# A Mamba block with a mixture of experts: the last chunk's rows in expert tiles, four running sums, and short chunks scanned in pairs of blocks

## The chip, the core and the metric

The kernel runs on one core of a Trainium2 chip. The core has five engines with a queue of instructions each: PE (matrix products), DVE (VectorE), ACT (ScalarE), POOL (GpSimd) and SP (SyncE, which here only issues DMAs). They run side by side and meet at semaphores. Sixteen DMA engines move data between HBM and the on-chip memory SBUF. The metric is the device time of one execution in microseconds; lower is better.

## What is computed

For 4096 rows of 256 values: a Mamba layer with residual and layer norm, then an expert layer with residual and layer norm. Cut to what matters (plain numpy shapes: L = 4096, D = 256, inner width 512, 16 states, 32 experts of width 128, 6 per row):

```python
# Mamba: project, causal convolution of 4 taps, silu, then the scan
dt = softplus(x_conv @ W_dt.T + b_dt)
Bm, Cm = x_conv @ W_B.T, x_conv @ W_C.T          # 16 values a row each
def step(h, inp):                                # h: [512, 16]
    h = exp(dt_t[:, None] * A) * h + dt_t[:, None] * B_t * u_t[:, None]
    return h, h @ C_t                            # y_t
x = layernorm(x + (y * silu(z)) @ W_out.T)

# experts: softmax router, the best 6 of 32, weights scaled to a sum of 1
shared = silu(x @ sg.T) * (x @ su.T) @ sd.T
for e in the six experts of a row:
    out_row += weight[row, e] * (silu(gate_e @ row) * (up_e @ row)) @ down_e
x = layernorm(x + out + shared)
```

All arithmetic is float32.

## The kernel before

**Chunks.** The rows are cut into nine chunks (`SIZES`, L92): a short one of 256 rows, seven of 512, a short one of 256. The channel axis lies on the partitions in four blocks `m` of 128, so a scan unit is one state and one block: `units` (L935) lists chunk, group `g` of two blocks, state `n`, block `i`. A chunk has 64 units.

**One unit** (the loop at L1031): ACT writes the decay `exp(dt * A)` into a PSUM tile `h` (`exp_at`, L961, two units ahead), POOL writes `du` = `u` times the row `b` (`du_at`, L953, four units ahead), DVE scans along the rows (L1066, start value `hlast`) and multiplies by the row `c` (L1070, into `hc`), PE adds `hc` to `y` through a transposing product (`summed`, L980), ACT keeps the last column for the next chunk (`keep`, L972). SP fetches rows `b` and `c` broadcast to all partitions (`load_bc`, L941), two pairs of units ahead.

**Threads.** All else runs as Python generators in `threads`; each unit calls `step()`, which advances every thread to its next `yield`. So the order of instructions on each engine is fixed when the program is built, and a thread's work is spread over the units. Beside the units of chunk `c` run: `front(c + 1)` (projections, convolution, `dt`), `tail(c - 1)` (gate, `W_out`, norm, then `prepare`: router, top 6, shared expert), and expert tiles of chunk `c - 2`.

**Tiles.** `ranked` (L395) gives each (row, expert) a place in a list of tiles of 128 rows, each of one expert; `copies` (L521) issues on POOL six indirect DMAs per 128 rows, which put the rows into the DRAM list `xs`. `SLOTS` (L108) is the number of tiles that the list needs at most, `full[c]` (L113) how many are surely full after chunk `c`; `stage(c)` (L693) lists the tiles that become full then. `tiles` (L671) starts a pair of tiles every `gap` steps; `loaded` (L566) issues its DMAs on SP (rows `xt`, weights `wt`, and expert weights `gu`, `dn`), `pair` (L643) or `pair_of` (L1110) computes it: transpose, gate and up product, tanh, down product, and `added` (L625): ACT scales the result by the row's weight (`yt`, two buffers), and POOL adds it to the output rows in DRAM by an indirect DMA that accumulates. Adds to one copy of the sums must follow each other, so there are three copies, `acc[0..2]` (`LANES`, L102), taken in turn: L635, `acc[(j + i) % LANES]`. `prepare` writes the shared expert's result plus the residual into `acc[0]` (L389). `blanked` (L239) and `cleared` (L252) write zeros into `xs` and `acc` beforehand.

**The last chunk** does not go through tiles. After the scan, `fw.wall` (L1108) takes the weights of all 32 experts (`walls`, L1202). Tiles of chunk 7 that are left are `EARLY` = 8 pairs with weights of their own, and 36 pairs that read from `wall` at an index held in a register. `dense` (L1214) runs every expert over all 256 rows of the last chunk (`expert`, L1176), with the weight of each row, broadcast by `weights` (L1149), zero where the expert was not chosen; it stops at expert 14 (`HALF`) until the tiles are done.

**The finish** (`finish`, L1236) takes two chunks at a time: three loads per chunk from the three copies, two DVE additions, the norm, a store. The next two chunks' loads are issued after the stores.

**PSUM.** Tiles for PE results come from `bank()`, three banks (`BANKS`); `room()` makes a thread wait at build time until one is free.

Of the kernel before, what the change touches and what calls it, by code (L numbers as in the profile page):

```python
# [60 lines left out]
def kernel(  # L61
# [32 lines left out]
    AT = [sum(SIZES[:c]) for c in range(NC)]  # L94
# [7 lines left out]
    LANES = 3  # L102

    AHEAD = 2
    BANKS = 3


    SLOTS = (L - SIZES[-1]) * TOP_K // P + E - 1  # L108
# [3 lines left out]

    full = [max(0, (AT[c + 1] * TOP_K // P - (E - 1)) // 2 * 2) for c in range(NC - 1)]  # L113
    full[NC - 2] = SLOTS

# [13 lines left out]
    held = [0]  # L129

    def room():
        while held[0] >= BANKS:
            yield

    def bank(name):
        held[0] += 1
        return ps_m.tile([P, T], F32, tag="mm", name=name)
# [3 lines left out]

    threads = []

# [85 lines left out]

    xs = dr1.tile([(SLOTS + 1) * P, RW], F32, tag="xs", name="xs")  # L230
    acc = [dr1.tile([L + P, D], F32, tag=f"acc{i}", name=f"acc_{i}") for i in range(LANES)]

    def bound(c):

        return AT[c + 1] * TOP_K // P + E - 1 if c < NC - 2 else SLOTS + 1

# [30 lines left out]
    def prepare(c):  # L267
# [69 lines left out]
        if c < NC - 1:  # L337
            yield from ranked(c, mask)
# [31 lines left out]
        if c == NC - 1:  # L370
            return
# [23 lines left out]
    def ranked(c, mask):  # L395
# [31 lines left out]
        if c < NC - 2:  # L427
            nc.vector.tensor_scalar(down, pc, -half, BIG, ALU.add, ALU.add)
            nc.vector.tensor_scalar_add(down, down, -BIG)
        else:  # L430
            nc.vector.tensor_copy(down, up)
# [89 lines left out]
    def copies(c, at):  # L521

        row, n = row_of[c], 0
        for b in range(blocks(c)):
            for k in range(TOP_K):
                yield
                n += 1
                if n % 3 == 0:
                    yield
                i = nc.gpsimd.indirect_dma_start(  # L530
# [77 lines left out]
    def turned_rows(j, xt):  # L608
        yield from room()
# [15 lines left out]
    def added(j, po, wt, no):  # L625

        yt = q2.tile([P, 2, D], F32, tag="yt", name=f"yt_{j}")
# [4 lines left out]
        for i in range(2):  # L632
            yield
            a = nc.gpsimd.indirect_dma_start(  # L634
                out=acc[(j + i) % LANES],  # L635
                out_offset=bass.IndirectOffsetOnAxis(ap=no[:, i : i + 1], axis=0),
                in_=yt[:, i, :],
                in_offset=None,
                compute_op=ALU.add,
            )  # L640
            adds.append(a.ins)

    def pair(j, xt, wt, gu, dn):  # L643
# [4 lines left out]
        for h in range(2):  # L648
            for i in range(2):
                for k in range(KD):  # L650
# [3 lines left out]
                    )  # L654
        yield
# [10 lines left out]
        for i in range(2):  # L666
            nc.tensor.matmul(po[:, i, :], hm[:, i, :], dn[i], start=True, stop=True)  # L667
        yield
        yield from added(j, po, wt, no)

    def tiles(c, gap, js, weights, one):  # L671
# [3 lines left out]
        if c == NC - 2:  # L675
            yield from rounds(4)
        st, going = {}, []
        for i in range(len(js) + AHEAD if js else 0):

# [17 lines left out]
    EARLY = 8  # L697


    with ExitStack() as c1:  # L700
# [4 lines left out]
        qw = c1.enter_context(tc.tile_pool(name="qw", bufs=6))  # L705
# [41 lines left out]
        nc.vector.memset(hlast, 0.0)  # L747

# [139 lines left out]
        def tail(c):  # L888
# [45 lines left out]

        units = [  # L935
            (c, g, n, i) for c in range(NC) for g in range(G) for n in range(NS)
            for i in range(2)
        ]
        PER = G * NS * 2

        def load_bc(s, which):  # L941
            if s >= len(units) // 2:
                return
            c, g, n, _ = units[2 * s]
            t = p3.tile(
                [P, T], F32, tag="bc"[which] + "b", name=f"{'bc'[which]}b_{c}_{g}_{n}"
            )[:, : SIZES[c]]
            nc.sync.dma_start(
                t, bcd_of[c][2 * n + which : 2 * n + which + 1, :].partition_broadcast(P)
            )  # L950
            (c_of if which else b_of)[s] = t

        def du_at(q):  # L953
            if q >= len(units):
                return
            c, g, n, i = units[q]
            du = p3.tile([P, T], F32, tag="du", name=f"du_{q}", bufs=6)[:, : SIZES[c]]
            nc.gpsimd.tensor_mul(du, u_of[c][:, 2 * g + i, :], b_of[q // 2])  # L958
            du_of[q] = du

        def exp_at(q):  # L961
            if q >= len(units):
                return
            c, g, n, i = units[q]
            m = 2 * g + i
            h = ps_a.tile([P, T], F32, tag="h", name=f"h_{q}")[:, : SIZES[c]]
            nc.scalar.activation(  # L967
                h, dt_of[c][:, m, :], AF.Exp, scale=aneg[:, m, n : n + 1]
            )
            h_of[q] = h  # L970

        def keep(q):  # L972
            c, g, n, i = units[q]
            if c + 1 < NC:
                m = 2 * g + i
                nc.scalar.copy(hlast[:, n, m : m + 1], h_of[q][:, SIZES[c] - 1 : SIZES[c]])  # L976
# [3 lines left out]
        def summed(q):  # L980

            c, g, n, i = units[q]
            nb = blocks(c)
            if n == 0 and i == 0:
# [5 lines left out]
            for b in range(nb):  # L990
                nc.tensor.matmul(  # L991
                    y_of[c, g][b // 2][:, b % 2, ts(i, P)], hc[:, ts(b, P)], ident,
                    start=(n == 0 and i == 0 and b % 2 == 0),
                    stop=(n == NS - 1 and i == 1 and b % 2 == 1),
                    is_transpose=True,
                )
# [32 lines left out]
        exp_at(1)  # L1029
        load_expert_constants()  # L1030
        for q, (c, g, n, i) in enumerate(units):  # L1031
            if q % PER == 0:
# [11 lines left out]
                if 0 < c < NC - 1:  # L1044
# [4 lines left out]
                if c == NC - 1:  # L1049
                    early = tiles(NC - 2, 3, stage(NC - 2)[:EARLY], qw, pair)  # L1050
# [3 lines left out]
            if q % 4 == 0 and 0 < c < NC - 1:  # L1054
# [10 lines left out]
            m = 2 * g + i  # L1065
# [3 lines left out]
            hc = p3.tile([P, T], F32, tag="hc", name=f"hc_{q}", bufs=6)[:, : SIZES[c]]  # L1069
            nc.vector.tensor_mul(hc, h, c_of[q // 2])  # L1070
            hc_of[q] = hc

            if q and n == 0 and i == 0:
# [4 lines left out]
            if q > 1 and n == 0 and i == 1:  # L1078
# [4 lines left out]
            if q % PER == PER - 6:  # L1083
                drain(*mains)
            if q % PER == PER - 1 and 0 < c < NC - 1:
# [7 lines left out]
        drain(last_tail, late, early)  # L1093
# [3 lines left out]
    f2 = ctx.enter_context(tc.tile_pool(name="f2", bufs=2))  # L1097
    f3 = ctx.enter_context(tc.tile_pool(name="f3", bufs=3))
    ps_o = ctx.enter_context(tc.tile_pool(name="ps_o", bufs=1, space=PSUM))
    ps_g = ctx.enter_context(tc.tile_pool(name="ps_g", bufs=3, space=PSUM))  # L1100
    EG = 4
    last = NC - 1
    nb, Tc = blocks(last), SIZES[last]
    row, x1T, hms = row_of[last], x1T_of[last], hms_of[last]
    sums = [ps_o.tile([P, T], F32, tag=f"o{b}", name=f"o_{b}")[:, :D] for b in range(nb)]

    GU = KD * 2 * P
    wall = fw.tile([P, E, GU + D], F32, tag="wall", name="wall")  # L1108

    def pair_of(j, xt, wt, es, _):  # L1110
# [4 lines left out]
        for i in range(2):  # L1115
            for k in range(KD):
# [4 lines left out]
                )  # L1121
        yield
# [22 lines left out]
        yield from added(j, po, wt, no)  # L1145

    columns, through = {}, []

    def weights():  # L1149

        yield from room()
        pw = bank("pw")
        for b in range(nb):
            nc.tensor.transpose(pw[:E, ts(b, P)], row[:, b, WT:RW], ident)
        yield
        ct = f2.tile([E, T], F32, tag="ct", name="ct", bufs=1)[:, :Tc]
        nc.scalar.copy(ct, pw[:E, :Tc])
        free()
        yield
        cd = dram.tile([E, T], F32, tag="cd", name="cd", bufs=1)[:, :Tc]  # L1160
        nc.sync.dma_start(cd, ct)
        yield
        for e in range(0, E, EG):
            while e >= 3 * EG and e - 2 * EG - 1 not in done_with:
                yield
            cb = f2.tile([P, EG, T // 2], F32, tag="cb", name=f"cb_{e}", bufs=3)
# [171 lines left out]
```

## Time and profile before

| | us |
|---|---|
| runs of the kernel (three) | 1987.65 median, 1987.5 to 1989.53 |
| profiled execution, device time | 1985.42 |
| its span, first to last instruction | 1983.7 |

Busy time over that span:

| engine | busy us | share |
|---|---|---|
| PE matmul | 1431.5 | 72% |
| PE weight load | 1025.8 | 52% |
| DVE | 1509.9 | 76% |
| ACT | 995.2 | 50% |
| POOL | 1185.7 | 60% |

The DMA queues moved 362.98 MB; q1 (issued by SP) took 54.1% of the sixteen engines' time and q0 (issued by POOL) 14.7%. The scan of the first short chunk begins at 47.4 us, that of the first long one at 157.3, that of the last short one at 1475.9; the last scan starts at 1632.3. The `W_out` product of the last chunk ends at 1640.9. The first add of the 36 last pairs starts at 1737.4, the last add lands at 1875.4.

A profile row of a group reads: line, engine, operation, output and inputs with shapes, count; then busy time and the mean of one in ns; then the time that the engine stood idle just before, and for what. A row of a window reads: the window and its length, then busy time and count per engine, the clock granted to PE (1 is full), the share of the DMA engines in use and the bytes per second. A group of a helper's line can mix shapes; a chain of waits lists, in order of time, start and length of each piece that held up the next.

### The profile page before, as it was taken

The page shows a single profiled execution, that of the slowest core. Times are in us where ns is not written, and L with a number is a line of the kernel's source. Part 1 is how long each engine was busy: PE and PEld are TensorE (multiplying, and loading weights), DVE is VectorE, ACT ScalarE, POOL GpSimd, SP SyncE. Part 2 cuts the span into 40 slices and gives each one's busy share as a digit, 9 for nine tenths or more (in the row PEclk, how much of TensorE's full clock was granted, in tenths as well). Part 3 has the DMA queues.
Part 4 walks back from the last instruction along what each step waited for, and adds up shares of the span by engine and source line. Part 5 has one row for each costly group of instructions (what it writes and reads, how often), then busy time and mean ns, then how long its engine had stood idle before and what let it go on. Part 6 is the DMA issues. An engine that isn't in the chain of part 4 may idle for free. (4 is left out here: it accounts for less than half of the span.)

```text
span 1983.7 us, 25634 instructions
## 1 busy us (share of the span) xinstructions
PE 1431.5 (72%) x6674; PEld 1025.8 (52%) x6674; DVE 1509.9 (76%) x2572; ACT 995.2 (50%) x2220; POOL 1185.7 (60%) x986
## 2 busy tenths in 40 slices
PE   5958556874876598669866987586656658899745
PEld 4325334533544365456545655575545547777544
DVE  3598899899889989996999799889977752322265
ACT  4566454644555465555654565455545324155333
POOL 1345556467556756795688568957884784087600
PEclk8868775985897599879887999798878879999877
DMA  8329535444744597778786878687857879988753
GB/s 238 82 74 327 163 109 179 131 110 150 220 114 126 171 267 183 210 168 255 194 204 171 249 207 214 173 241 209 234 132 202 194 165 245 296 144 137 133 185 112
DMA packets 334978, 362.98 MB, mean 183 GB/s; under 512 B 64816, under 2 KB 270480, under 8 KB 334832
## 3 DMA queue, kind: packets, MB, share of 16 engines
q1 hardware_dynamic: 293552, 306.85, 54.1%
q0 software_dynamic: 39168, 54.45, 14.7%
q8 instruction: 54, 0.88, 0.2%
q14 instruction: 92, 0.75, 0.1%
q10 hardware_dynamic: 2112, 0.05, 0.1%
HBM read 257.80 MB, written 103.42 MB: 182 GB/s over the span
## 5 line engine op out<-in xcount | busy, mean ns | idle before, releaser
L958 POOL TENSOR_TENSOR du<-u,bb 128x512 f32<-128x512 f32 (+1 forms) x576 | 716.0, 1294 | 447.6 <-DVE h L1066 245.1
L1066 DVE TENSOR_TENSOR_SCAN h<-h,hlast,du 128x512 f32<-128x512 f32 (+1 forms) x576 | 671.0, 1165 | 52.1 <-POOL du L958 25.9
L991 PE MATMUL y<-ident,hc 128*128 128x128 f32 x2048 | 380.8, 321 | 205.6 <-DVE hc L1070 199.2
L991 PEld LDWEIGHTS y<-ident,hc 128*128 128x128 f32 x2048 | 284.9, 165 | 328.4 <-DVE hc L1070 256.3
L1070 DVE TENSOR_TENSOR hc<-h,cb 128x512 f32<-128x512 f32 (+1 forms) x576 | 364.4, 633 | 98.1 <-DMA cb<-bcd 52.0
L634 POOL DMA_INDIRECT acc<-yt,no x212 | 334.3, 1577 | 168.6 <-ACT yt L629 104.3
L967 ACT ACTIVATE h<-dt,aneg 128x512 f32<-128x512 f32 (+1 forms) x576 | 370.8, 644 | 70.9 <-DVE hc L1070 51.0
L976 ACT COPY hlast<-h 128x1 f32<-128x1 f32 x512 | 80.8, 158 | 424.2 <-DVE hc L1070 423.5
L530 POOL DMA_INDIRECT xs<-row,at x180 | 187.3, 1041 | 70.9 <-issue 35.0
L667 PE MATMUL po<-dn,hm 128*128 128x256 f32 x280 | 91.9, 459 | 137.2 <-issue 73.6
L651 PE MATMUL pg<-xsT,gu 128*128 128x128 f32 x1120 | 152.1, 294 | 4.2 <-ACT xsT L617 4.2
L651 PEld LDWEIGHTS pg<-xsT,gu 128*128 128x128 f32 x1120 | 148.9, 212 | 8.9 <-ACT xsT L617 4.7
L667 PEld LDWEIGHTS po<-dn,hm 128*128 128x128 f32 x280 | 57.6, 222 | 165.0 <-issue 85.5
L629 ACT ACTIVATE yt<-po,wt 128x256 f32<-128x256 f32 x212 | 88.2, 467 | 82.4 <-DMA acc<-yt,no 56.1
L829 PE MATMUL pd<-u,w_dt 128*128 128x512 f32 (+1 forms) x288 | 120.4, 564 | 1.0 <-ACT e L835 1.0
L793 PE MATMUL pv<-xin,taps 128*128 128x512 f32 (+1 forms) x288 | 117.5, 551 | 1.7 <-ACT hlast L976 1.5
L1126 DVE SCALAR_TENSOR_TENSOR gt<-gt,pg 128x256 f32<-128x256 f32 x36 | 15.2, 422 | 104.0 <-ACT gt L1124 101.3
L614 PE MATMUL pt<-ident,xt 128*128 128x128 f32 x424 | 66.6, 280 | 22.7 <-DVE row L929 5.5
L829 PEld LDWEIGHTS pd<-u,w_dt 128*128 128x128 f32 x288 | 54.8, 197 | 49.6 <-issue 44.3
L1174 PE MATMUL o<-wall,hm_all 128*128 128x256 f32 x128 | 38.9, 434 | 57.3 <-DVE hm_all L1195 57.3
L793 PEld LDWEIGHTS pv<-xin,taps 128*128 128x128 f32 x288 | 52.8, 192 | 45.5 <-issue 40.3
L782 PE MATMUL px<-xT,w_in 128*128 128x512 f32 (+1 forms) x144 | 69.3, 609 | 6.0 <-DVE row L929 5.3
(205 smaller groups left out, 2067.2 us busy)
## 6 DMA issues: line engine op xcount, KB each, us to landing
bb<-bcd SPq DMA_DIRECT2D x224, 256.0 KB
cb<-bcd SPq DMA_DIRECT2D x224, 256.0 KB
gu<-in_gate_up_t_dram SPq DMA_DIRECT2D x140, 256.0 KB
xs<-blank SPq DMA_DIRECT2D x52, 578.0 KB
xt<-xs SPq DMA_DIRECT2D x212, 128.5 KB
dn<-in_down_t_dram SPq DMA_DIRECT2D x140, 128.0 KB
out<-acc SPq DMA_DIRECT2D x21, 512.0 KB
bb<-bcd SPq DMA_DIRECT2D x64, 128.0 KB
```

The lines of the kernel that those rows point to most:

```text
L530: i = nc.gpsimd.indirect_dma_start(out=xs, out_offset=bass.IndirectOffsetOnAxis(ap=at[:, b, k : k + 1], axis=0), in_=row[:, b, :], in_offs ...
L629: nc.scalar.mul(yt[:, i, :], po[:, i, :], wt[:, i : i + 1])
L634: a = nc.gpsimd.indirect_dma_start(out=acc[(j + i) % LANES], out_offset=bass.IndirectOffsetOnAxis(ap=no[:, i : i + 1], axis=0), in_=yt[:, ...
L651: nc.tensor.matmul(pg[:, h, i, :], gu[i][:, k, ts(h, P)], xT[:, i, k, :], start=(k == 0), stop=(k == KD - 1),)
L667: nc.tensor.matmul(po[:, i, :], hm[:, i, :], dn[i], start=True, stop=True)
L793: nc.tensor.matmul(pv, taps[:, m, k, :], xin[:, m, k : k + Tc], start=(k == 0), stop=(k == TAPS - 1),)
L829: nc.tensor.matmul(pd, w_dt[:, k, ts(m, P)], u[:, k, :], start=(k == 0), stop=(k == M - 1),)
L958: nc.gpsimd.tensor_mul(du, u_of[c][:, 2 * g + i, :], b_of[q // 2])
L967: nc.scalar.activation(h, dt_of[c][:, m, :], AF.Exp, scale=aneg[:, m, n : n + 1])
L991: nc.tensor.matmul(y_of[c, g][b // 2][:, b % 2, ts(i, P)], hc[:, ts(b, P)], ident, start=(n == 0 and i == 0 and b % 2 == 0), stop=(n == NS ...
L1066: nc.vector.tensor_tensor_scan(h, h, du_of.pop(q), hlast[:, n, m : m + 1], ALU.mult, ALU.add)
L1070: nc.vector.tensor_mul(hc, h, c_of[q // 2])
```

## The change

Three things change at once.

1. **The last chunk's rows go to tiles like all others.** `ranked` and the shared expert's store run for every chunk; `SLOTS` and `full` cover all nine chunks. `weights`, `expert`, `dense` and `second` are gone. The tiles of chunk 7's stage all run as early pairs with weights of their own, and `pair_of` runs the pairs of the last stage.
2. **Four copies of the sums.** `added` takes a parameter `lane`: `pair` adds to copies 0 and 1, `pair_of` to copies 2 and 3. Beside the last tiles, `halfway` loads copies 0 and 1 and adds them into the SBUF tile `sums`. `finish` now takes four blocks of 128 rows, adds copies 2 and 3 (loaded into the space of `wall`), normalizes and stores; eight of these run staggered by one step.
3. **Short chunks scan two blocks in one instruction.** A unit of a short chunk covers both blocks of a group: 512 columns, the first block's 256 rows and then the second's. `joined` writes the second block's start into its first column (`du` becomes decay times `hlast` plus `du`, the decay becomes zero), so that the scan restarts there. A short chunk has 32 units, and each calls `step()` twice.

Smaller edits: `take` and `give` count buffers in use when the program is built; the end of the scan waits for the `W_out` product and for chunk 6's tiles only, so that weight loads mix with early pairs; five more PSUM banks serve the last stage; a put of `copies` waits for another POOL instruction since the put before, or issues a tiny `memset` (`apart_from`); chunk 7's puts lose their extra `yield`.

```diff
-    LANES = 3
+    LANES = 4
-    SLOTS = (L - SIZES[-1]) * TOP_K // P + E - 1
+    SLOTS = L * TOP_K // P + E - 1
...
-    full = [max(0, (AT[c + 1] * TOP_K // P - (E - 1)) // 2 * 2) for c in range(NC - 1)]
-    full[NC - 2] = SLOTS
+    full = [max(0, (AT[c + 1] * TOP_K // P - (E - 1)) // 2 * 2) for c in range(NC)]
+    full[NC - 1] = SLOTS
...
-        if c < NC - 1:
-            yield from ranked(c, mask)
+        yield from ranked(c, mask)
...
-                if n % 3 == 0:
+                if n % 3 == 0 and c < NC - 2:
                     yield
+                while apart_from[0] and c < NC - 1:
+                    yield
+                if apart_from[0]:
+                    nc.gpsimd.memset(between, 0.0)
+                apart_from[0] = True
...
-    def added(j, po, wt, no):
+    def added(j, po, wt, no, lane):
+        yield from take("yt", 2)
...
-                out=acc[(j + i) % LANES],
+                out=acc[lane + (j + i) % 2],
...
+        def joined(q):
+            if q >= len(units) or not short(units[q][0]):
+                return
+            n, m, k = state(q)
+            Tc = SIZES[units[q][0]]
+            first, du = h_of[q][:, Tc : Tc + 1], du_of[q][:, Tc : Tc + 1]
+            nc.scalar.activation(
+                du, first, AF.Identity, bias=du, scale=hlast[:, n, m + 1 : m + 2]
+            )
+            nc.scalar.copy(first, zero)
...
-                    early = tiles(NC - 2, 3, stage(NC - 2)[:EARLY], qw, pair)
+                    early = tiles(NC - 2, 3, stage(NC - 2), qw, pair)
...
             nc.vector.tensor_tensor_scan(
                 h, h, du_of.pop(q), hlast[:, n, m : m + 1], ALU.mult, ALU.add
             )
-            nc.vector.tensor_mul(hc, h, c_of[q // 2])
+            joined(q + 2)
+            if short(c):
+                step()
+            nc.vector.tensor_mul(parts(q, hc), parts(q, h), row_for(q, 1))
...
-        drain(last_tail, late, early)
+        while NC - 1 not in z_done or late in threads:
+            step()
...
+    pools += [ctx.enter_context(tc.tile_pool(name="ps_n", bufs=MORE, space=PSUM))] * MORE
...
+    sums = fw.tile([P, L // P, D], F32, tag="sums", name="sums")
...
+    FEW, MANY = 2, 4
+    def halfway():
+        while early in threads or last_tail in threads:
+            yield
+        for b in range(0, L // P, FEW):
+            other = qw.tile([P, FEW, D], F32, tag="gu", name=f"other_{b}")
+            nc.sync.dma_start(sums[:, b : b + FEW, :], rows_of(acc[0], b, FEW))
+            nc.sync.dma_start(other, rows_of(acc[1], b, FEW))
+            yield from rounds(6)
+            nc.vector.tensor_add(sums[:, b : b + FEW, :], sums[:, b : b + FEW, :], other)
+    def finish(b):
+        part = wall[:, b : b + MANY, :].rearrange("p e i -> p (e i)")
+        part = part[:, : 2 * MANY * D].rearrange("p (l b d) -> p l b d", l=2, d=D)
+        for i in range(2):
+            nc.sync.dma_start(part[:, i], rows_of(acc[2 + i], b, MANY))
+        yield
+        whole = sums[:, b : b + MANY, :]
+        for i in range(2):
+            nc.vector.tensor_add(whole, whole, part[:, i])
+        yield from normalize([sums[:, b + i, :] for i in range(MANY)], f"f{b}")
+        yield
+        nc.sync.dma_start(rows_of(out, b, MANY), whole)
+    def finishes():
+        while rest in threads or half in threads:
+            yield
+        yield from beside([finish(b) for b in range(0, L // P, MANY)], 1)
...
-        yield from tiles(NC - 2, 3, stage(NC - 2)[EARLY:], None, pair_of)
+        yield from tiles(NC - 1, 3, stage(NC - 1), None, pair_of)
...
-    threads += [walls(), weights(), dense(), rest, finishes()]
+    rest, half = last_tiles(), halfway()
+    threads += [walls(), rest, half, finishes()]
```

## The prediction

> **What bounds the kernel now.** I first cut the span into stages, by the lines that run in each: short chunk 0 (47 to 157 us), long chunks 1 to 7, short chunk 8 (1476 to 1634), the stage that loads all expert weights (to 1722), the last tiles (to 1876), the finish. The view of busy time by window, columns as its second line names them:
>
> ```profile
> core 0 of [0], span 1983.7 us
> core 0: us, PE busy (x) PEld busy (x) DVE busy (x) ACT busy (x) POOL busy (x), PEclk, DMA share, GB/s
> 47.00:157.00 110.00, 76.68 (x222) 34.36 (x222) 83.68 (x146) 64.99 (x162) 47.01 (x64) 0.73 0.31 84
> 1476.00:1541.00 65.00, 48.28 (x262) 41.25 (x262) 47.22 (x126) 32.40 (x70) 32.33 (x38) 0.81 0.72 188
> 1541.00:1634.00 93.00, 54.20 (x279) 42.59 (x277) 59.29 (x129) 30.07 (x75) 75.65 (x75) 0.78 0.77 177
> 1641.00:1722.00 81.00, 67.66 (x369) 58.85 (x368) 28.48 (x83) 25.22 (x64) 24.64 (x16) 0.94 1.00 277
> 1737.00:1876.00 139.00, 129.01 (x642) 99.99 (x640) 29.91 (x71) 75.42 (x210) 111.00 (x72) 0.99 0.83 132
> 1876.00:1984.00 108.00, 49.57 (x188) 40.74 (x188) 58.76 (x148) 32.89 (x61) 0.00 (x0) 0.74 0.48 156
> ```
>
> Each stage has its own limit. VectorE is fullest in chunk 0; POOL is in the second half of chunk 8 (76 of 93); the DMA engines are full (1.00) while weights load; POOL and PE share the last tiles; in the finish nothing is full, so that stage is a chain of waits: load, add, normalize, store, next pair of chunks.
>
> The last tiles need a closer look: 72 adds in 139 us. POOL is busy 1.54 us per add, and the timeline of POOL shows 0.30 between two, so one add per 1.85 us, 3.75 us per pair with its few waits. How long an add is on its way, by the chain of waits and the view of the line in 1737:1876, and what share of the DMA engines the adds (q0) and the tile loads (q1) take in 1740:1845:
>
> ```profile
> 1783.77 3.83 DMA acc<-yt,no
> 1787.90 4.26 DMA acc<-yt,no
> 1824.07 5.89 DMA acc<-yt,no
> DMA to landing us min/median/max: 3.6/4.2/4.6
> q0 software_dynamic: 8007, 7.30, 53.5%
> q1 hardware_dynamic: 16911, 7.72, 34.6%
> ```
>
> An add lands some 4.2 us after its start; 13 such pieces of the chain average 4.16. With three copies the same copy comes up every 5.5 us, so POOL waits rarely (5.7 us in ten waits). Per pair the adds cost 2.0 us of all DMA engines (53.5% of 105 us over 56 adds is 1.0 each), the loads 1.25.
>
> **1. The dense path goes, the finish is pipelined.** Before, 32 experts run over the last chunk: 14 in the shadow of the weight loads, 18 in gaps of the finish. Neither sets a stage's length; what their end frees is the finish's order. After: all 32 row blocks are finished in eight groups of four, one group's loads beside another's arithmetic. VectorE per group: two 128x1024 adds at 1.23 to 1.30, four bn_stats with aggregate at 0.53, 0.5 of small operations: 5.1 us. DMA per group: two 512 KB loads and one store, 1.5 MB, 4.5 us at the 350 GB/s that the finish's bursts show. VectorE leads: 5.5 us to the first pair of loads, 8 x 5.1 = 41, then 0.4, four scalings at 0.5, a store at 3.5, 1 of end: 54 us for 108. **-54** (bounds -48 to -57). Two of the four copies are read and added before: see 3.
>
> **2. More tiles, later start.** Slots go from 212 to 224. By the formula of `full`, the last stage has 148..224, 38 pairs for 36; the stage before has 12 pairs, all with weights of their own, where 8 were early. So the weight stage carries four pairs more: 8 x 512.5 KB at 288 GB/s (5.9 MB in 66% of 31 us at 1641:1672) is 14.6 us of DMA; 8 adds at 0.92 (18.2% of 81 us over 16), 7.4; twelve puts of chunk 8, 7; the eight 512 KB broadcasts of weights go, four of them here, -6. 81 + 23 = 104, of which the engines' overlap (shares up to 1.06) takes back some: 100, **+19**. SP issues less than that: 64 weight loads at 0.48, 80 tile loads at 0.58, five list reads at 2: 87 us. In the new order the load of the last chunk's `row` stands before the early tiles in SP's queue, and waits until the last put of chunk 7 has landed; behind it wait all early loads and then the weights, which before began at 1630. **+6** (0 to +10). From the last weight to the first add: 15.4 before, about 14: -1.
>
> **3. Two copies for the last tiles.** Before, adds go round three copies; after, even slots go to one copy and odd ones to the other, and the last stage uses copies 2 and 3 alone, so that copies 0 and 1 can be summed beside it. An add waits for the one two places before it: queued behind on POOL are only adds, behind those the scaling on ACT (`yt` has two buffers), then PSUM and PE. The rule that speaks against the change is the row: 4.2 us of landing for a copy that returns after 3.7. The Trainium skill, "DMA: Bandwidth & Descriptors", section "Anatomy of one DMA", fits such a DMA as 2.0 us and bytes over 436 GB/s; for 128 KB that is an estimate of 2.3 us, under 3.7: then two copies are enough and a pair stays at 3.75. By the row a pair takes 4.2 and the hand-over (0.1 to 0.7 from a landing to the next start, 0.2 taken). I take the row. Then the half sums: 16 times 2 x 256 KB, 1.5 us of all DMA engines each, every second pair, so 4.0 us of DMA per pair in 4.4, share 0.9, as at 1737:1782; for their bursts 0.2. Pair: **4.6** (bounds 3.75, POOL alone; 5.3, the landing of 5.1 at 1645:1690, where the DMA share is 1.0). First add to last landing: 37 x 4.6 + 6 = 176, before 1737.4 to 1875.4, 138: **+38** (+7 to +64). SP per pair: four loads at 0.58, list reads 1, half sums 0.5: 3.85, covered. PE 3.6, covered. VectorE's 16 adds (0.69): in 139 us it is busy 30, covered.
>
> **4. Two blocks at once in the short chunks.** The view of groups, shapes apart (count, busy, mean ns):
>
> ```profile
> L958 POOL TENSOR_TENSOR du<-u,bb 128x512 f32<-128x512 f32 x448 | 612.3, 1417 | 319.4 <-DVE h L1066 182.6 <-DMA bb<-bcd 113.6 <-DVE hc L1070 15.5
> L1066 DVE TENSOR_TENSOR_SCAN h<-h,hlast,du 128x512 f32<-128x512 f32 x448 | 574.8, 1283 | 15.8 <-POOL du L958 10.7 <-ACT hlast L976 2.1 <-ACT h L967 2.0
> L1070 DVE TENSOR_TENSOR hc<-h,cb 128x512 f32<-128x512 f32 x448 | 310.0, 692 | 68.3 <-DMA cb<-bcd 32.1 <-DVE h L1066 2.8 <-PE y L991 1.1
> L1066 DVE TENSOR_TENSOR_SCAN h<-h,hlast,du 128x256 f32<-128x256 f32 x128 | 96.2, 751 | 36.3 <-POOL du L958 15.2 <-ACT h L967 11.1 <-ACT hlast L976 9.3
> L1070 DVE TENSOR_TENSOR hc<-h,cb 128x256 f32<-128x256 f32 x128 | 54.4, 425 | 29.8 <-DMA cb<-bcd 19.9 <-PE spo L378 0.2
> ```
>
> Two short units cost VectorE 2 x 1.18 = 2.35, one double unit 1.283 + 0.692 = 1.97: 0.4 less, 32 times a chunk. In chunk 0 only the part from 100 us on is VectorE's (before it PE is busy 46 of 53 us with the next front): some 18 doubles, -7. In chunk 8's first half 15 doubles, -6, and the b and c rows, fetched four units ahead, now have 7.9 us of cover for 4.7, which shortens the DMA waits (cb 19.9, bb 15.1 us in the chunk): -5. The second half is POOL's: a group of three puts, two adds and four `du` takes 10.2 us; with two double `du` 3 x 1.0 + 2 x 1.6 + 2 x 1.42 and gaps, less the overlap of an add with the `du` behind it, 10.3. 24 puts are eight groups either way: -1. The joining adds two one-column ACT operations per double unit (0.16 to 0.2 each, against one saved copy): +6 us of ACT a chunk, hidden, ACT is busy 65 of 110; but the scan waits for them, +0 to +5 if ACT's queue is blocked. Together **-19** (0 to -35).
>
> **5. Small ones.** The fourth copy is cleared in chunk 1: 4.3 MB, 12 us more of a DMA share of 1.07; VectorE there is busy 0.90 against 0.95: **+2** (0 to +6). 14 more blank tiles in chunk 8 at share 0.75: 0 to +4, taken 0.
>
> **Sum:** -54 + 19 + 6 - 1 + 38 - 19 + 2 = **-9**. Against the profiled execution (1985.42, span 1983.7) this is 1976; the median of the runs is 2.2 above that execution: **1978**. Two big terms, -54 and +62 (parts 2 and 3), nearly cancel, so small errors decide the sign; 0.2%, 4 us, is what can be told from no change.
>
> **Rivals.** B, the copies don't hold POOL up: landings fall below 3.7 because fewer adds are under way (3.6 at 1850:1876, where no tile loads remain). A pair takes 3.75, the last tiles 145 us: -31, **1947**. Against it: 3.9 to 4.5 in all windows with tile loads. C, slower: the half sums fill the DMA engines and the landing is that of 1645:1690, a pair takes 5.4, the last tiles 206 us: +30, **2008**. For it: ten waits of POOL show landings of 5.9 already now. It decides from 4.85 us per pair on (4.6 + 9/37). D, the short chunks gain nothing, because POOL in chunk 8 and PE in chunk 0 hold the pace and the joining costs what VectorE saves: **1997**.
>
> **Numbers.** A (1978, own range 1963 to 1992) 0.45: of it 0.32 faster, 0.08 same, 0.05 slower. B 0.20, faster. C 0.27, D 0.08, slower. Faster 0.52, same 0.08, slower 0.40. Range 1942 to 2012: B's and C's times with a few us of the other bounds.
>
> **What would show it.** Adds to copies 2 and 3 spaced in pairs of 4.6 with POOL waiting on `DMA acc<-yt,no` near 0.8 us per pair (B: none; C: over 1.5); first of them some 120 us after the `w_out` product of the last chunk ends (before 96); 54 us from the last landing to the end; chunk 0 at 103 us, chunk 8 at 146. I am wrong if the last tiles run at POOL's 1.85 per add, or the finish takes over 65.

## The result, and the profile after

The changed kernel is slower: 2021.16 us median of four runs (2018.33 to 2026.95) against 1987.65. The ratio is 1.017, with a 95% interval of 1.0147 to 1.0194, so the loss is 1.7% and clear of the noise. I had forecast 1978 and a range up to 2012, so both the sign and the range are wrong. The profiled execution has a span of 2025.2 us, 41.5 more than before (its time lies some 6 us above the median of its runs; the stages below are those of the profiled executions).

The span cut into stages, by the first scan of a chunk, the last scan, the first add of the last tiles, the landing of the last add, and the end:

| stage | before | changed | difference | forecast |
|---|---|---|---|---|
| start to first scan | 47.4 | 50.0 | +2.6 | 0 |
| chunk 0 | 109.9 | 108.1 | -1.8 | -7 |
| chunks 1 to 7 | 1318.6 | 1329.3 | +10.7 | +2 |
| chunk 8, first to last scan | 156.4 | 141.7 | -14.7 | -12 |
| last scan to first add of the last tiles | 105.1 | 148.9 | +43.8 | +24 |
| first add to last landing | 138.0 | 194.9 | +56.9 | +38 |
| last landing to end | 108.3 | 52.3 | -56.0 | -54 |
| sum | 1983.7 | 2025.2 | +41.5 | -9 |

The busy time by window of the changed kernel; the windows are chunk 0, the two halves of chunk 8's scan, the weight load, what follows it, the last tiles and the finish:

```profile
core 0: us, PE busy (x) PEld busy (x) DVE busy (x) ACT busy (x) POOL busy (x), PEclk, DMA share, GB/s
50.00:158.00 108.00, 70.90 (x218) 35.96 (x218) 76.07 (x82) 74.00 (x184) 41.11 (x32) 0.74 0.26 81
1487.00:1553.00 66.00, 47.34 (x256) 39.67 (x257) 45.87 (x100) 40.45 (x105) 35.73 (x27) 0.77 0.89 239
1553.00:1629.00 76.00, 51.01 (x281) 42.40 (x279) 50.70 (x91) 35.30 (x100) 57.78 (x47) 0.82 0.73 176
1643.00:1722.00 79.00, 39.76 (x172) 33.91 (x173) 19.48 (x91) 15.11 (x39) 26.89 (x25) 0.63 0.98 292
1722.00:1776.00 54.00, 37.50 (x196) 31.64 (x195) 8.18 (x19) 15.10 (x42) 21.24 (x14) 0.84 0.74 160
1776.00:1973.00 197.00, 139.03 (x649) 104.14 (x648) 40.09 (x88) 73.33 (x220) 119.25 (x77) 0.94 0.76 140
1973.00:2025.00 52.00, 0.00 (x0) 0.00 (x0) 39.06 (x104) 18.14 (x40) 0.00 (x0) 0.50 0.75 240
```

Read the last two rows against those of before. The finish now has VectorE at 39 of 52 us: the chain of waits is gone, and a busy engine sets the length. In the last tiles POOL was 111 of 139 us busy; now it is 119 of 197, and nothing else is near full. A stage in which no engine is full is again a chain of waits, and the view of the sums' copies in 1776:1973 names it (who idled for what: us, times):

```profile
L658 POOL DMA_INDIRECT acc<-yt,no x77: 1546/1550/1564, 1776.1 to 1969.3; - x77
  DMA acc<-yt,no: 51.6, 35
  ACT yt L652: 18.3, 28
  ACT yt L652: 69.3, 23
```

The 38 last pairs make 76 adds, from 1778.0 us on; the 77th, at 1776.1, is the last one of the early pairs. The second and third line are POOL's idle time: 51.6 us for landings and 18.3 for ACT's scaling. The last line is of the list of those who waited for the landings: ACT stood 69.3 us before a scaling, because the two buffers of `yt` come back only when their adds have landed, too. Before, POOL waited 5.7 us for landings in this stage, and ACT 35.0.

The groups that answer to those shown of before, and the joining operation that is new (count, busy, mean ns, idle before):

```profile
L1019 POOL TENSOR_TENSOR du<-u,bb 128x512 f32<-128x512 f32 x512 | 701.0, 1428 | 438.0 <-DVE h L1156 234.0 <-DMA bb<-bcd 148.5 <-DVE hc L1163 29.8
L1156 DVE TENSOR_TENSOR_SCAN h<-h,hlast,du 128x512 f32<-128x512 f32 x512 | 656.8, 1283 | 45.7 <-ACT h L1047 23.2 <-POOL du L1019 17.9 <-ACT hlast L1057 2.4
L1163 DVE TENSOR_TENSOR hc<-h,cb 128x512 f32<-128x512 f32 x512 | 354.0, 691 | 71.6 <-DMA cb<-bcd 30.1 <-PE y L1076 1.8 <-PE px L950 1.6
L1044 ACT ACTIVATE du<-h,du,hlast 128x1 f32<-128x1 f32 x64 | 22.5, 351 | 17.8 <-POOL du L1019 12.6
```

A double scan costs what was assumed, 1283 and 691 ns. The joining column takes 351 ns where I had 160 to 200, and the scan waits 23.2 us in all for the second half of the joining (`h` L1047, the zero), 21.0 of them in chunk 0. But the scans of chunk 0 waited for ACT before, too, for `keep` and for the decay. Who the scans waited for in chunk 0 (us, times), two lines of before and one of the changed kernel:

```profile
  ACT hlast L976: 9.3, 6
  ACT h L967: 7.7, 4
  ACT h L1047: 21.0, 6
```

So the scans of this chunk wait 4.0 us more for ACT than they did, which lies inside the "+0 to +5" of step 4.

### The profile page after: what moved, and what is told of

It is laid out like the page before. It is cut to its first block, busy times and chain, and to the rows that moved or that the text cites. A ratio compares the mean times of both kernels' runs of the same rounds, so it can differ in the third digit from the quotient of the medians.

```text
span 2025.2 us, 24981 instructions
## 1 busy us (share of the span) xinstructions
PE 1390.3 (69%) x6426; PEld 994.1 (49%) x6426; DVE 1480.9 (73%) x2435; ACT 1008.3 (50%) x2309; POOL 1209.0 (60%) x950
## 5 line engine op out<-in xcount | busy, mean ns | idle before, releaser
L1019 POOL TENSOR_TENSOR du<-u,bb 128x512 f32<-128x512 f32 x512 | 701.0, 1428 | 438.0 <-DVE h L1156 234.0
L1156 DVE TENSOR_TENSOR_SCAN h<-h,hlast,du 128x512 f32<-128x512 f32 x512 | 656.8, 1283 | 45.7 <-ACT h L1047 23.2
L658 POOL DMA_INDIRECT acc<-yt,no x224 | 354.4, 1582 | 238.2 <-ACT yt L652 96.2
L1163 DVE TENSOR_TENSOR hc<-h,cb 128x512 f32<-128x512 f32 x512 | 354.0, 691 | 71.6 <-DMA cb<-bcd 30.1
L551 POOL DMA_INDIRECT xs<-row,at x192 | 199.8, 1041 | 84.9 <-issue 37.3
L676 PEld LDWEIGHTS pg<-xsT,gu 128*128 128x128 f32 x1184 | 171.5, 227 | 9.6 <-DMA gu<-in_gate_up_t_dram 2.7
L676 PE MATMUL pg<-xsT,gu 128*128 128x128 f32 x1184 | 173.8, 309 | 2.6 <-DMA gu<-in_gate_up_t_dram 2.4
L1216 DVE SCALAR_TENSOR_TENSOR gt<-gt,pg 128x256 f32<-128x256 f32 x38 | 16.0, 421 | 145.6 <-ACT gt L1214 131.7
L687 DVE SCALAR_TENSOR_TENSOR gt<-gt,pg 128x256 f32<-128x256 f32 x74 | 30.6, 414 | 109.8 <-ACT gt L684 76.2
L636 PEld LDWEIGHTS pt<-ident,xt 128*128 128x128 f32 x448 | 55.3, 147 | 85.6 <-issue 50.5
L639 ACT COPY xsT<-pt 128x512 f32<-128x512 f32 x112 | 65.8, 588 | 52.9 <-PE pt L636 51.5
```

The lines of the kernel that those rows point to most:

```text
L551: i = nc.gpsimd.indirect_dma_start(out=xs, out_offset=bass.IndirectOffsetOnAxis(ap=at[:, b, k : k + 1], axis=0), in_=row[:, b, :], in_offs ...
L636: nc.tensor.transpose(pt4[:, i, k, :], xt[:, i, ts(k, P)], ident)
L658: a = nc.gpsimd.indirect_dma_start(out=acc[lane + (j + i) % 2], out_offset=bass.IndirectOffsetOnAxis(ap=no[:, i : i + 1], axis=0), in_=yt[ ...
L676: nc.tensor.matmul(pg[:, h, i, :], gu[i][:, k, ts(h, P)], xT[:, i, k, :], start=(k == 0), stop=(k == KD - 1),)
L1019: nc.gpsimd.tensor_mul(parts(q, du), u, row_for(q, 0))
L1156: nc.vector.tensor_tensor_scan(h, h, du_of.pop(q), hlast[:, n, m : m + 1], ALU.mult, ALU.add)
```

## The experiments

Times of the kernel before, measured anew beside each group of runs: 1990.4, 1995.1, 1999.9 and 1987.2 us. So what is compared across groups are ratios to the kernel before, and stages of the profiles.

In what follows "a pair" is the time from one add to the next but one, taken over the whole stage: first to last add over 37.5 intervals in kernels with 38 pairs. It is 5.10 us in the changed kernel (191.3 us) and 3.79 before (134.4 us over 35.5).

### A third copy for the last tiles

```diff
-    LANES = 4
+    LANES = 5
-                out=acc[lane + (j + i) % 2],
+                out=acc[lane + (j + i) % ways],
...
-        yield from added(j, po, wt, no, 2)
+        yield from added(j, po, wt, no, 2, 3)
...
-        for i in range(2):
-            nc.sync.dma_start(part[:, i], rows_of(acc[2 + i], b, MANY))
+        for i in range(3):
+            nc.sync.dma_start(part[:, i], rows_of(acc[2 + i], b, MANY))
```

> A fifth copy: the last tiles' adds go round copies 2, 3 and 4 in turn, everything else as in the changed kernel; the finish reads and adds one copy more. Theory W (an add waits for the copy to come back): the pair of tiles falls from 5.2 to about 3.9 us, the last tiles from 197 to about 150 us, the finish grows by 8 x 1.23 = 10 us; time about 1983 us. Rival Q (the transfers of the half sums and tile loads, or SP's queue, hold the pair, whatever the number of copies): the pair stays at 4.8 us or above, time 2015 us or more.

Measured: 2002.0 us, ratio 1.006 (1.0041 to 1.0079). The copies in the last tiles, with POOL's wait for landings:

```profile
L658 POOL DMA_INDIRECT acc<-yt,no x77: 1545/1549/1990, 1776.2 to 1926.8; - x77
  DMA acc<-yt,no: 7.3, 11
```

As above, the first of the 77 adds is an early one. A pair takes 3.97 us, the last tiles 152 us for 195, the finish 65 for 52. Both terms came near those of theory W, though the time lies 19 us above its 1983: the theory's terms make -37, the two profiled executions differ by -29.5 us, the medians by -19. Rival Q falls: with the half sums and all loads still there, one more copy takes 1.1 us out of each pair, and POOL's wait for landings falls from 51.6 us to 7.3.

### Two copies in the kernel before

```diff
-    LANES = 3
+    LANES = 2
```

> The kernel before with two copies of sums instead of three, nothing else; its finish loads and adds one copy less. Theory W: the pair of last tiles goes from 3.75 to 4.9 or 5.1 us, 36 pairs give 41 to 48 us, chunks 1 to 7 about 6 us more, the finish 10 to 15 us less; 1.6 to 2.2% slower than the kernel before, whose last tiles have no half sums and no other new work beside them. If two copies are enough (landing hidden), it is 10 us faster than the kernel before.

Measured: 2024.2 us, ratio 1.0149 (1.0094 to 1.0203), a little less than theory W had.

```profile
L634 POOL DMA_INDIRECT acc<-yt,no x72: 1540/1540/1558, 1749.2 to 1918.2; - x72
  DMA acc<-yt,no: 27.5, 22
```

A pair takes 4.76 us (169.0 us over 35.5), the finish 97 us for 108. One character in the old kernel makes about the same loss as the whole change. Chunks 1 to 7 take 1319.4 us: no loss there.

### The half sums later

```diff
     def halfway():
-        while early in threads or last_tail in threads:
+        while early in threads or last_tail in threads or rest in threads:
             yield
```

> The sums of copies 0 and 1 begin only when the last tiles are done; two copies for the last tiles as in the changed kernel. Theory W: the pair still waits for its copy, 4.5 to 4.8 us, last tiles about 178 us, then some 28 us of half sums by themselves (16 x 1.75); time about 2030 us. Rival Q: the pair falls to 4.0 us or below without the half sums' transfers, last tiles about 153; time about 2005 us.

Measured: 2022.0 us, ratio 1.0168 (1.0144 to 1.0193): no change. The half sums now run from 1922 to 1965, in the last quarter of the tiles, since SP has then issued the tile loads. The adds until they begin:

```profile
L658 POOL DMA_INDIRECT acc<-yt,no x62: 1545/1549/1563, 1774.8 to 1918.6; - x62
  DMA acc<-yt,no: 19.7, 21
```

The median pair of these is 4.71 us, where the changed kernel has 5.12 (1800 to 1925). From 1922 on, with the half sums one behind the other, it is 7.4, and the stage is about as long as in the changed kernel (192 us for 195). So the half sums add some 0.4 us to a pair that they run beside; the rest of the pair's growth is the two copies: theory W's pair holds, rival Q's falls.

Why 4.7, where the landing takes about 4 us? The chain of waits of the changed kernel, in the last pairs, where no loads are left (start, length, what):

```profile
1953.91 3.61 DMA acc<-yt,no
1957.56 0.69 issue
1958.26 3.71 DMA acc<-yt,no
1962.01 0.69 issue
1962.70 3.72 DMA acc<-yt,no
1966.46 0.69 issue
```

Each landing is followed by 0.69 us before the next add starts. By the landings in the traces' semaphore events, 59 of 74 adds of the changed kernel start 0.73 us after the landing of the add two places before, and 48 of 70 in the old kernel with two copies. One whose copy is free follows its predecessor after 0.30, and one that had to wait for ACT's scaling starts 0.28 after that (the first add of the last tiles before, at 1737.4). So the 0.7 goes with a wait for a landing, not with any wait; what makes it stays open. A copy returns after landing plus 0.7: 4.4 here (3.7), 4.7 with tile loads (4.0), 5.0 with half sums beside them (4.3), where a mean pair takes 5.2, since a quarter of the adds wait for more than their copy. I had seen hand-overs of 0.1 to 0.7 and taken 0.2.

### Four copies, all in turn, no half sums

The same edits as for three copies below, with `LANES = 4`.

> As the kernel with three copies and no half sums, but with four copies, adds round all four in every stage, and a finish that loads four. Theory W: three copies already hide the landing, so the pair of last tiles stays at 3.8 us; the finish grows by 8 x 1.2 to 10 us; time about 1979 us. For the 6 to 9 us in chunks 1 to 7: if they belong to a fourth copy as such (its memory, its clearing), these chunks take 1326 us or more here; if they belong to adds that share two copies, 1321 us.

Measured: 1978.5 us, ratio 0.9952 (0.9932 to 0.9972). A pair takes 3.77 us, where three copies (below) take 3.81, and the finish 63 us for their 56: a fourth copy gains next to nothing in the tiles and costs 7 us in the finish.

### Three copies, no half sums

```diff
-    LANES = 4
+    LANES = 3
-                out=acc[lane + (j + i) % 2],
+                out=acc[(j + i) % LANES],
-    def halfway():
...
     def finish(b):
+        nc.sync.dma_start(whole, rows_of(acc[0], b, MANY))
-        for i in range(2):
-            nc.sync.dma_start(part[:, i], rows_of(acc[2 + i], b, MANY))
+        for i in range(LANES - 1):
+            nc.sync.dma_start(part[:, i], rows_of(acc[1 + i], b, MANY))
```

> Three copies in all stages, adds round all three as before the change; no sums beside the last tiles, the finish loads three copies per group of four row blocks and adds two. All else as in the changed kernel. Theory W (the two copies cost the last tiles 5.2 against 3.75 to 4.0 us per pair, and the long chunks 6 to 9 us, since the adds there use two copies as well): last tiles about 150 us for 197, chunks 1 to 7 back at 1320 us for 1329, finish 57 to 62 us for 52; time about 1972 us. If the long chunks stay at 1327 and only the last tiles gain: 1980 us. If the pair stays above 4.6: over 1995 us.

Measured: 1970.0 us, ratio 0.9876 (0.9835 to 0.9917): with the pipelined finish and three copies in turn as before, the change is a gain of 1.2%. Its copies in the last tiles, and its last tiles and finish by window:

```profile
L658 POOL DMA_INDIRECT acc<-yt,no x76: 1547/1549/1565, 1768.2 to 1911.0; - x76
  DMA acc<-yt,no: 2.2, 3
DMA to landing us min/median/max: 3.8/4.6/5.3
```

```profile
1768.00:1915.00 147.00, 128.26 (x648) 100.15 (x646) 30.29 (x72) 77.27 (x219) 117.73 (x76) 0.97 0.88 129
1915.00:1971.00 56.00, 0.00 (x0) 0.00 (x0) 39.20 (x104) 18.13 (x40) 0.00 (x0) 0.50 0.91 299
```

POOL waits 2.2 us for landings although these take 4.6 in the median: three copies return after 3 x 1.85 = 5.5 us, and that covers 4.6 + 0.7. A pair takes 3.81 us. The finish, with a third more to move, takes 56 us for 52: the half sums beside the tiles, for which the fourth copy was added, save 4 us there.

### Weights behind the early tiles

```diff
     def walls():
+        while early in threads or last_tail in threads:
+            yield
         for e in range(E):
```

> The 64 weight loads are put behind the early tiles and the last chunk's tail in SP's queue, as before the change; the rest as in the changed kernel. Theory O (the early pairs are slow because the weight loads are woven between their loads): early pairs fall from 9.6 to about 5 us, the last of the weights lands about 1745 instead of 1722, but the first add of the last tiles comes about 1757 instead of 1776; time about 2002 us. Rival V (the bytes of that stage set its length, in whatever order): 2017 to 2025 us.

Measured: 2036.8 us, ratio 1.0237 (1.0217 to 1.0258). The edit did more than was meant by it. SP's timeline (start, length, line, operation):

```profile
1715.53 0.48 SPq L1242 DMA_DIRECT2D wall<-in_gate_up_t_dram  x1
1716.06 0.51 SPq L1246 DMA_DIRECT2D wall<-in_down_t_dram  x1
1735.71 0.37 SPq L1263 DMA_DIRECT2D sums<-acc  x1
1737.71 0.37 SPq L1264 DMA_DIRECT2D other<-acc  x1
1738.13 0.46 SPq L1242 DMA_DIRECT2D wall<-in_gate_up_t_dram  x1
```

The half sums wait on the same condition, so their first load (L1263) got into SP's queue behind the fourth weight load. It waits until the early adds have landed, and sixty weight loads wait behind it for 20 us. The order alone was tried with three copies and no half sums, by the same three lines:

> As the kernel with three copies and no half sums, and the weight loads are put behind the early tiles and the last chunk's tail in SP's queue. Without half sums nothing stands before the weights that waits for an early add. Theory O: early pairs fall from 9.6 to 5 to 6 us, the weights are issued from about 1700 and land by 1745, the first add of the last tiles comes at about 1757 instead of 1776; time 15 to 20 us under the run without this edit, about 1955 us. Rival V (the bytes set the length): within 5 us of it, about 1972 us.

Measured: 1970.4 us, ratio 0.9872 (0.9841 to 0.9903), as without the edit. Theory O is half right: the early adds end at 1733.5 instead of 1765. But the weights then end later (last issue 1753 for 1709), and the first last pair comes 132 us after the first early load, for 137 without the edit. Rival V holds: the order is worth nothing in the time, and 5 us in this stage of the profiles.

### The base store on another queue

```diff
-            i = nc.sync.dma_start(
+            i = (nc.scalar if c == NC - 1 else nc.sync).dma_start(
```

> The changed kernel with one edit: the store of the last chunk's base rows into copy 0 is issued on ACT's queue instead of SP's, where it stood behind the loads of the early tiles and of the first last tiles. Theory S (adds to copy 0 wait for that store, 11.6 us of POOL's time, and the early pairs end later for it): the store is issued near 1744 instead of 1755, the first add of the last tiles comes 8 to 11 us earlier; time about 2011 us. Rival (the early pairs are held by their own loads, so the wait only shows there): 2018 to 2022 us.

Measured: 2022.3 us, no change in the time (2021.16). The 11.6 us wait, which POOL had at 1758 for `acc<-base` behind SP's queue, is gone, and the stage from the first early load to the first last pair takes 129 us for 135, of which the time shows nothing. The wait was mostly a symptom: without it POOL waits for the early pairs themselves.

### All remaining pairs on the resident weights

```diff
-                if c == NC - 1:
-                    early = tiles(NC - 2, 3, stage(NC - 2), qw, pair)
-                    threads.append(early)
...
-        yield from tiles(NC - 1, 3, stage(NC - 1), None, pair_of)
+        yield from tiles(NC - 2, 3, stage(NC - 2) + stage(NC - 1), None, pair_of)
```

(and the edits of three copies without half sums; at the first tile of the last stage `tiles` waits until chunk 8's rows are put)

> As the kernel with three copies and no half sums, and the 12 pairs of the stage before go with the last 38 through the resident weights, so that they load none of their own (12 x 768 KB less) and start after the weight load. Theory B (the stage behind the scan is bound by bytes and by SP's queue, the last tiles by POOL at 3.75 to 3.9 us per pair): weights land about 1690, then 50 pairs in 190 us, finish 60; time about 1945 us. Rival P (a pair on resident weights takes 4.3 or more, or the last chunk's tail holds the first pairs): 1970 us or more.

Measured: 1951.9 us, ratio 0.9778 (0.9746 to 0.981), the fastest of all. Its windows, from the last scan to the first add, the 50 pairs, the finish:

```profile
1620.00:1699.00 79.00, 30.74 (x112) 23.49 (x112) 20.12 (x89) 11.55 (x26) 22.46 (x31) 0.65 0.81 220
1699.00:1896.00 197.00, 172.46 (x864) 134.49 (x862) 40.37 (x96) 102.27 (x291) 154.76 (x100) 0.97 0.86 128
1896.00:1951.00 55.00, 0.00 (x0) 0.00 (x0) 39.19 (x104) 18.13 (x40) 0.00 (x0) 0.50 0.92 304
```

The stage behind the scan shrinks from 151 us (the three-copy kernel) to 79, while twelve pairs more on resident weights take 12 x 3.9 = 47. A pair takes 3.90 us, and theory B holds within 7 us. This run moves the twelve pairs and drops their loads at once; it does not tell which of the two gives how much.

### Short chunks with single blocks

```diff
         def short(c):
-            return SIZES[c] < T
+            return False
```

(and tiles cut to the chunk's 256 columns), in the changed kernel and in the kernel with all pairs on resident weights:

> Short chunks scan one block at a time, as before the change; the rest as in the changed kernel. If the double blocks gave what the two profiles differ by in the two short chunks (109.9 to 108.1 and 155.2 to 141.7 us, 15 together): time about 2036 us. If that difference came from elsewhere in chunk 8 (the early tiles, the puts' order): 2021 us.

> As the kernel with all remaining pairs on resident weights, with short chunks scanned one block at a time. Theory G (the double blocks shorten the last scan by 16 us, and this passes through to the end where the weight load follows the scan directly; in the changed kernel it does not, because the row load and the early tiles behind it wait for the last puts, which did not move forward): 12 to 18 us slower than with double blocks, about 1967 us. Rival (the double blocks gain nothing for the end whatever follows them): within 4 us of 1952.

Measured: 2017.4 us in the changed kernel, which has 2021.2 with double blocks; 1962.8 on resident weights (ratio 0.9823, 0.9782 to 0.9864), which has 1951.9 (0.9778). So the double blocks gained nothing in the changed kernel. The times below count from the first scan of chunk 8:

| | last scan | last put of chunk 7 | first early load | first add of the last stage |
|---|---|---|---|---|
| before | 156.4 | 151.5 | 154.5 | 261.5 |
| changed | 141.7 | 150.7 | 155.7 | 290.6 |
| changed, single blocks | 158.7 | 134.5 | 143.9 | 285.3 |
| resident, double | 141.8 | 150.8 | none | 221.0 |
| resident, single | 154.9 | 137.3 | none | 230.7 |

The double blocks bring the last scan 17 us forward, the last put 16 us back and the first early load 12 us back. The reason for the put, by the code: a put waits for another POOL operation since the put before, and there are half as many `du` to stand between; no run took that rule away. In the changed kernel the next stage begins with loads that wait for those puts, so the scan's gain ends there. The load of the last chunk's `row` heads SP's queue, and the view of SP's waits in 1620:1656 (us in total, times, longest) has it:

```profile
SPq L923 <- DMA xs<-row,at: 27.0, 2, 24.0
```

On resident weights the weight load follows the scan directly, and 10 of the 13 us pass through, a little less than theory G had; the intervals of the two ratios overlap, so this rests on the stages of the two profiles, not on the times.

### The kernel before, once more

> The kernel before, profiled once more, to see how far the length of chunks 1 to 7 varies between executions. If it is 1320 us within 3, the 6 to 9 us that the changed kernel and its variants have there are the change's; if it comes out at 1326 or more, they are not.

Measured: chunks 1 to 7 take 1324.3 us, between the two cases, and 5.6 us more than in the first profile of the same kernel. Over all profiles these chunks take 1317.6 to 1324.3 us in the two of the kernel before, in its two-copy form, and in the changed forms whose adds go round all copies; and 1326.1 to 1330.7 in the six kernels that keep early adds to copies 0 and 1 beside further copies. The groups don't overlap, and 8 us lie between their means, little more than between two profiles of one kernel. Two copies alone don't do it (1319.4), nor do four as such (1317.6). The instruction order in these chunks is the same on PE, VectorE, ACT and POOL in the changed kernel and in that with four copies in turn. The clock granted to PE there is 0.821 in the mean of the six and 0.826 in that of the others, but 0.821 in the 1324.3 us profile, too; whether it is cause or companion is not shown. What makes the difference stays open.

## Why the prediction failed

1. **Finish: right.** -56 for -54, with VectorE leading as worked out.
2. **Two copies: the mechanism right, the size wrong (+56.9 for +38).** I weighed the row (4.2 us of landing) against the estimate of 2.3 for 128 KB, from the fit of the Trainium skill ("DMA: Bandwidth & Descriptors", "Anatomy of one DMA"), and took the row. No landing in the lines shown is under 3.6, and the two-copy runs in both kernels show that this choice was right and that rival B falls. Two terms of the step were too small. "The hand-over (0.1 to 0.7 ..., 0.2 taken)" is 0.7 whenever the add waits for a landing, and with two copies most adds do. "For their bursts 0.2" is 0.4 to 0.5. The landing itself was a little shorter than taken, 4.0 beside tile loads. Together that is 5.1 for 4.6, over 37 pairs 19 us, all that this stage missed. The pair lay in my bounds (5.3) and beyond the 4.85 from which rival C decides; POOL's wait of 1.4 us per pair lies between my 0.8 and C's 1.5. But C's cause, half sums that fill the DMA engines, is the smaller part: without them a pair still takes 4.7, and the DMA share in the last tiles is 0.76, lower than before.
3. **Weight stage: +43.8 for +24.** The first add of the last tiles comes 139 us after the last `W_out` product, where I had 120. Of the 20 us missed, 10 belong to the start: the step gave the early loads 6 us for the wait behind chunk 7's puts, but took the puts to end earlier with the faster scan. They don't, so the first early load comes 155.7 us after chunk 8's first scan, as before (154.5), and a scan that ends 15 us sooner only lengthens the gap behind it. That is also why step 4 failed at the end: it was right about the scan (-14.7 for -12 in chunk 8), and wrong that the end would follow. I had costed POOL's groups of three puts, and called it "-1", but not what waits for the last put. Another 10 us: from first early load to first last pair 135 us, before 107, where bytes gave 18 more. The DMA share is 0.98 until 1722, as computed, and then 0.74 for 54 us: after the weights have landed, early pairs are still under way, each behind its own loads. The weights' place in the queue and the base store give 5 to 6 us of this stage each in the profiles and nothing in the time (two runs); taking the early pairs off this stage gives 25, what they cost later deducted. (The step counted 80 tile loads for SP where the 24 early tiles take four each, 96; SP's issue time is then 96 us for 87, still under the 104 of the bytes.)
4. **Chunk 0: -1.8 for -7.** The step split the chunk rightly: its first 26 scans of before are not VectorE's, the rest are. The rest, 18 doubles, went from 56.7 us to 52.3, -4.4 for -7, since VectorE's work for the next front took 16.0 us beside them for 13.4. The first part, which the step put at nothing, grew from 53.2 us to 55.8: scans and front wait there for ACT, which the joining keeps busier (74 us of the chunk for 65). No run took the joining alone away; single blocks in the changed kernel give the same chunk within 0.5 us.
5. **Chunks 1 to 7: +10.7 for +2.** The clearing of the fourth copy costs nothing (chunk 1 takes 172.7 us in both). The rest is the open 8 us.

The forecast's chances had slower at 0.40. Its weakness was that it summed two large terms of opposite sign, and set the range as if one of them would miss: two of its terms came some 20 us too long each, and their errors added up.

## What to carry to other kernels

When operations of one queue go round n buffers, compare n times the issue interval with the landing *plus the time from a landing to the start that waits for it*, and take that time from the longest such gap in the chain of waits: a queue that must wait each time pays it each time. A stage made shorter moves the end only if what starts the next stage moves too: look for the last operation that the next stage's first load waits for, and ask whether the change brings it forward or back. Work put beside another stage to save time at the end must be weighed against the resources it takes from that stage: here the last tiles gave up one of three copies for 4 us of finish, and that cost over 40.

## What the runs showed beyond that

- POOL's add starts 0.69 us after the landing that it waits for, 0.28 after an ACT scaling that it waits for, and 0.30 after the add before it when all is ready.
- An add's landing is not a constant: 3.7 us with no loads beside; in the two three-copy kernels, whose last tiles run the same instructions, the medians of the landings that the profile tells are 4.6 and 3.9.
- A 128 KB tile load issued right behind the 12.6 MB of weights took 11.7 us (in the chain of waits of the kernel on resident weights). Moving that load ahead of the last weights would be the next thing to try; no run did it.
